# A decoder layer on one core: batch 0's shared expert in seven block products, and two sets of sums given out elsewhere

## The chip, the cores and the metric

The kernel runs on one core of a Trainium2 chip. The core has TensorE (PE, matrix products), VectorE (DVE), ScalarE (ACT) and GpSimd (POOL) for elementwise work, and queues of transfers that SyncE (SP), ScalarE and GpSimd issue. The metric is the device time of one execution in microseconds, as a median over several runs. The profile is of one more execution.

## The reference

A decoder layer on x of 4 batches x 512 tokens x 512 features, float32. Three blocks follow one another, each on the layer norm of x and added back to x:

```python
x = x + attention(_layernorm(x), wq, wk, wv, wo)       # 32 heads of 64, 8 key/value heads, causal
x = x + quantized_product(_layernorm(x), ctx_2048)     # both sides rounded to fp8 by blocks of 128
x = x + moe(_layernorm(x), Wg, W1, W3, W2, sw1, sw3, sw2)

def moe(xt, ...):                                      # xt: 2048 x 512
    probs = softmax(xt @ Wg)                           # 8 experts, the best one is taken
    # each expert takes its first 256 tokens, the rest are dropped
    h  = silu(xd @ W1[e]) * (xd @ W3[e])               # 512 -> 704, per expert
    oe = h @ W2[e]                                     # 704 -> 512
    shared = silu(xt @ sw1) * (xt @ sw3) @ sw2         # the same shape, for every token
    return gate * oe[slot] + shared
```

The change is in the last block only: the shared expert's upper part (silu(xt @ sw1) * (xt @ sw3)) and the sums around it.

## The kernel before

**Stages.** Attention of all four batches comes first (to about 1073 us). The quantized product and the routing of each batch are jobs that run beside it. Then comes the shared expert, batch by batch (to about 1300 us), with the last batch's quantized product and routing still beside it; then the eight experts (to 1532 us); then the last three pairs of shared lower products, beside which the experts' results are gathered and added.

**The shared expert.** Its upper part for batch b has six parts: chunks 0 to 4 of 128 hidden columns each (`HF` is 5), and a last one of 64 columns, here called (b,HF). `up` computes a chunk plainly: four products over k for sw1 into one PSUM bank and four for sw3 into another, each 128x128 by 128x512; then a silu on ScalarE and a product on VectorE. `up7` computes the same chunk in seven block products instead of eight, in the manner of Strassen and Winograd: the 2x2 blocks are (sw1, sw3) by halves of the 512 input features on the weights' side, and halves of the features by halves of the tokens on the other. A product has two matmuls 256 tokens wide. In order they are product 0 (a11 with b11), 1 (s2 with t2), 2 (s3 with t3), 3 (s1 with t1), 4 (a12 with b21), 5 (s4 with b22) and 6 (a22 with t4). VectorE joins them by seven additions, ScalarE copies one and takes two silus, and GpSimd multiplies the two results, called the gate product here.

The sums s1 to s4 of the weights come from `weight_sums` (four GpSimd instructions per chunk: s3, s1, s2, s4; s1 overwrites a21, the others go to `wS`, which is used again from expert to expert). The sums t1 to t4 of the tokens come from `token_sums` (GpSimd; for the last batch, t1, t2 and t4 on VectorE and t3 on GpSimd). In batch 0 every chunk is computed by `up`; after each, its weights' sums are formed for the batches behind it, and after chunk 2 the token sums of batch 1. `shared_down` computes 256 tokens of the lower part.

**Order of the work.** The schedule is manual: each engine executes what the program issues to it in that order. `units` lists the shared expert's units. Within a unit, `up`, `up7` and `down` call a function between their products (L1356, `between`), here called a stop: it advances the planner's clock `work.at` (1720 ns as a rule; 2500, 1700 and 1700 in `up7`) and then gives out steps of the jobs that are due. A job step that costs VectorE much names its price, and a stop has room for so much: 2.8 at the stops of `up` and `down`, and 1.3, 2.8 and 1.0 at the three of `up7`. Waits between steps are in units of `HALF`, 7250 ns of the planner's clock. A step marked "quiet" also waits until the planner reckons GpSimd done.

The jobs still open when the shared expert begins are, by the names of the code: r, m, n, o of the last heads (r broadcasts reciprocal row sums into `rrb` by a transfer, m and n multiply the heads' outputs aT by it on GpSimd in four instructions, and o is their output product, 16 matmuls, L408); c (rounding of the last batch's context, the transposes ptr_c); s and t (norm and quantized product of the last batch: a row h, a rounding, a transpose ptr_h, and four results y that GpSimd adds to acc); and w (the third norm, transposes ptr_h, router logits plg, the router, and four scatters of rows to `xd` by GpSimd). Expert e reads its 256 rows back from `xd` (`load_rows`, tile xe), transposes them (`turn_rows`, ptr_e) and forms their token sums (`expert_sums`).

**Experts.** For each of five chunks: `up7`, then `weight_sums` of the same chunk for the next expert; after chunk 1 the next expert's rows are turned, after chunk 2 its token sums are formed. Then `expert_rest` of the next expert (its 64-column part) and `down` of this one (products epy, chunk after chunk).

Of the kernel before, what the change touches and what calls it, by code (L numbers as in the profile page):

```python
# [11 lines left out]
ALU = mybir.AluOpType  # L12
# [11 lines left out]
def decoder_layer(  # L24
# [19 lines left out]
    B, T, D = x.shape  # L44
    HD = 64
    NQ = wq.shape[1] // HD
    E, _, H = W1.shape
# [7 lines left out]
    NHC = len(HCH)  # L55
# [39 lines left out]
    def bank(tag, name, dt=F32):  # L95
        bufs = {"sp": 4, "av": 1, "mm": 3}[tag]
        return psum.tile([P, 512], dt, tag=tag, bufs=bufs, name=name)
# [67 lines left out]
    def spin(n, name):  # L165
# [10 lines left out]
        out=mask[:, T - P : T],  # L176
# [19 lines left out]
        out=tri,  # L196
# [75 lines left out]
    def gpsimd(us, *args):  # L272
        nc.gpsimd.tensor_tensor(*args)  # L273
        work.gpsimd = max(work.gpsimd, work.at) + 1000 * us
# [474 lines left out]
    for b in range(B):  # L749
        z = b * SPB  # L750
# [329 lines left out]
    HF = H // P  # L1080
# [28 lines left out]
    se, h3x = {"next": 0}, {}  # L1109

    def load_h3(b):
        if b < B and b not in h3x and ("h3d", b) in over:
            h3x[b] = se[b % 2].tile([P, KC, T], F32, tag="h3x", name=f"h3x_{b}")
            bulk(out=h3x[b], in_=h3d[b])
# [17 lines left out]
    for d in range(len(todo)):  # L1132
# [12 lines left out]
        mid = work.spent  # L1145
# [12 lines left out]
    slots, evw = [], {}  # L1158
# [11 lines left out]
    gTs, xts = {}, {}  # L1170
# [6 lines left out]
    def up(w13, xT, gT, c, cols, name, mid=None):  # L1177


        at = (c * P, H + HT + c * P) if c < HF else (HF * P,)  # L1180
        ps = [bank("sp", f"p{m}_{name}") for m in range(len(at))]
        for pp, o in zip(ps, at):
            for k in range(KC):
                nc.tensor.matmul(  # L1184
                    pp[:, 0:cols],
                    w13[:, k, o : o + P],
                    xT[:, k, 0:cols],
                    start=(k == 0),
                    stop=(k == KC - 1),
                )  # L1190
                if mid and k % 2:
                    mid()
        g = gT[:, c, :]
        if c < HF:
            nc.scalar.activation(g, ps[0][:, 0:cols], AF.Silu)
            nc.vector.tensor_tensor(g, ps[1][:, 0:cols], g, ALU.mult)
            return

        nc.scalar.activation(g[HT:P, :], ps[0][0:HT, 0:cols], AF.Silu)
        gv = g.rearrange("p (a two t) -> p two a t", two=2, t=P)  # L1200
        pv = ps[0][:, 0:cols].rearrange("p (a two t) -> p two a t", two=2, t=P)
        nc.vector.tensor_tensor(gv[0:HT, 0], pv[HT:P, 0], gv[HT:P, 0], ALU.mult)
        nc.vector.tensor_tensor(gv[HT:P, 1], pv[HT:P, 1], gv[HT:P, 1], ALU.mult)
# [33 lines left out]
    xS = {}  # L1237

    def blocks(w, c):

        cols = slice(c * P, (c + 1) * P)
        low = slice(H + HT + c * P, H + HT + (c + 1) * P)
        return (
            w[:, 0:2, cols], w[:, 2:4, cols], w[:, 0:2, low], w[:, 2:4, low],
            *(wS[:, i, :, cols] for i in range(3)),
        )

    def weight_sums(w, c):

        a11, a12, a21, a22, s2, s3, s4 = blocks(w, c)  # L1250
        gpsimd(0.66, s3, a11, a21, ALU.subtract)
        gpsimd(0.66, a21, a21, a22, ALU.add)
        gpsimd(0.66, s2, a21, a11, ALU.subtract)
        gpsimd(0.66, s4, a12, s2, ALU.subtract)

    def token_sums(x, ts, cols, vector=False):

        half = cols // 2
        b11, b12, b21, b22 = (x[:, k : k + 2, t : t + half] for k in (0, 2) for t in (0, half))
        t1, t2, t3, t4 = ts  # L1260
        us = 1.27 * cols / T
        gpsimd(us, t3, b22, b12, ALU.subtract)
        for out, y, z in (t1, b12, b11), (t2, b22, t1), (t4, b21, t2):
            if vector:
                nc.vector.tensor_tensor(out, y, z, ALU.subtract)
            else:
                gpsimd(us, out, y, z, ALU.subtract)
        return t1, t2, t3, t4, b11, b21, b22

    def shared_sums(b):  # L1270
        xS[b] = token_sums(h3x[b], [xSs[:, i] for i in range(4)], T, b == B - 1)

    def up7(w, sums, g, c, cols, name, mid=None):
        a11, a12, s1, a22, s2, s3, s4 = blocks(w, c)
        t1, t2, t3, t4, b11, b21, b22 = sums
        half = cols // 2

        def product(i, w, x):
            ps = bank("av" if i == 3 else "sp", f"p7_{name}_{i}")[:, 0:half]
            for k in range(2):  # L1280
                nc.tensor.matmul(ps, w[:, k, :], x[:, k, :], start=k == 0, stop=k == 1)  # L1281
            return ps

        def part(tag, n=T // 2):
            return gp.tile([P, n], F32, tag=tag, bufs=2, name=f"{tag}_{name}")

        p1, u2, u3, c2 = part("p1"), part("u2"), part("u3"), part("c2", T)
        nc.scalar.copy(p1[:, 0:half], product(0, a11, b11))
        p1, u2, u3 = p1[:, 0:half], u2[:, 0:half], u3[:, 0:half]
        nc.vector.tensor_tensor(u2, product(1, s2, t2), p1, ALU.add)  # L1290
        nc.vector.tensor_tensor(u3, product(2, s3, t3), u2, ALU.add)
        if mid:
            mid(2500, 1.3)
        p5 = product(3, s1, t1)
        nc.vector.tensor_tensor(u2, p5, u2, ALU.add)
        nc.vector.tensor_tensor(c2[:, half:cols], p5, u3, ALU.add)
        nc.vector.tensor_tensor(g[:, 0:half], product(4, a12, b21), p1, ALU.add)
        if cols == T:
            nc.scalar.activation(g[:, 0:half], g[:, 0:half], AF.Silu)
        if mid:  # L1300
            mid(1700)
        nc.vector.tensor_tensor(g[:, half:cols], product(5, s4, b22), u2, ALU.add)
        lo = half if cols == T else 0
        nc.scalar.activation(g[:, lo:cols], g[:, lo:cols], AF.Silu)
        nc.vector.tensor_tensor(c2[:, 0:half], product(6, a22, t4), u3, ALU.add)
        gpsimd(1.27 * cols / T, g, g, c2[:, 0:cols], ALU.mult)
        if mid:
            mid(1700, 1.0)

    def shared_up(b, c, mid=None):  # L1310
        if b not in gTs:
            gTs[b] = gp.tile([P, NHC, T], F32, tag="gT", bufs=2, name=f"gT_{b}")
        if b and c < HF:
            up7(se["w"][0], xS[b], gTs[b][:, c, :], c, T, f"s{b}_{c}", mid)
        else:
            up(se["w"][0], h3x[b], gTs[b], c, T, f"s{b}_{c}", mid)
        if not b and c < HF:
            weight_sums(se["w"][0], c)
            if c == 2:
                shared_sums(1)  # L1320
        if c == (HF - 1 if b else HF):
            se["next"] = b + 2
            load_h3(b + 2)

# [22 lines left out]
    kept = set()  # L1347
    units = []
    for b in range(B):
        units += [(shared_up, b, c) for c in range(HF if b else NHC)]  # L1350
        units += [(shared_down, b, j) for j in range(0, TB, 2)]
        if b < B - 1:
            units.insert(-1, (shared_up, b + 1, HF))


    def between(ns=1720, room=2.8):  # L1356
        work.at += ns
        work.upto(n, 1e18, room)

    between()  # L1360
    while jobs or work.now:
        n += 1
# [20 lines left out]
    def load_w2(e):  # L1383
        if e < E:
            next(loads[e])
# [14 lines left out]
    def turn_rows(e):  # L1400
        if e < E:
            xTs[e] = h3x[B - 2][:, e % 2 * 2 : e % 2 * 2 + 2, :].rearrange(
                "p a (c t) -> p (a c) t", t=CAP
            )
            for t in range(CT):
                nc.scalar.copy(
                    xTs[e][:, :, t * P : (t + 1) * P],
                    transpose4(xes[e, t], f"ptr_e_{e}_{t}"),
                )
# [26 lines left out]
    units = [u for u in ups if u[2] == HF] + downs[:-3] + [u for u in ups if u[2] < HF]  # L1436
# [11 lines left out]
    units = downs[-3:]  # L1448
# [15 lines left out]
    for e in range(E):  # L1464
        for c in range(HF):
            up7(evw[e][0], exS[e], egTs[e][:, c, :], c, CAP, f"e{e}_{c}")
            if e < E - 1:
                weight_sums(evw[e + 1][0], c)
            if c == 1:
                turn_rows(e + 1)  # L1470
                load_rows(e + 2)
            if c == 2:
                expert_sums(e + 1)
        expert_rest(e + 1)
        load_e(e + 2)
        if e == E - 1:
            rows_back()
        for t, py in enumerate(down(egTs[e], evw[e][1], 0, f"epy_{e}", "mm")):
            yo = ep.tile([P, D], F32, tag="yo", bufs=2, name=f"yo_{e}_{t}")
            nc.vector.tensor_copy(yo, py)  # L1480
            r0 = e * CAP + t * P
            nc.sync.dma_start(out=oe[r0 : r0 + P, :], in_=yo)
        load_w2(e + 2)
# [96 lines left out]
```

## Time and profile before

| what | value |
|---|---|
| median of 3 runs | 1572.47 us (1570.51 to 1572.54) |
| profiled execution, its own time | 1569.79 us |
| span of that execution, first to last instruction | 1568.1 us |
| busy: TensorE, VectorE, ScalarE, GpSimd | 1530.8, 920.8, 535.1, 546.0 us |
| transferred | 194.42 MB, 124 GB/s on average |
| mean granted TensorE clock | 0.998 of full speed |

A row of a timeline is: start and length in us, engine, line (L273 is the helper through which all of GpSimd's elementwise instructions go), operation, output tile <- input tiles, shape, count; in brackets the idle time before it and what ended that. A 128x512 float32 product appears as two records. A stretch's row gives busy times of the five engines, the granted clock, the busy share of the transfer engines and GB/s.

### The profile page before, as it was taken

To read this page: it belongs to the slowest core of one execution; us is meant where nothing else is said; L and a number is where in the kernel's file an instruction comes from. 1 tells how busy PE (TensorE), PEld (TensorE's weight loads), DVE (VectorE), ACT (ScalarE), POOL (GpSimd) and SP (SyncE) were. 2 spreads that over 40 slices of the span, in tenths; PEclk is the share of its full clock that TensorE was granted. 3 is DMA by queue.
4 is the path that set the end of the run, shared out by engine and by line. 5 is a ranking of instruction groups with operands and counts; after the bars stand their busy time and mean duration, and the time that the engine had idled before them with its cause. 6 is when DMAs were issued, how large, how long until landed. Compare 5 with 4: busy or idle time off the path is not lost.

```text
span 1568.1 us, 22176 instructions
## 1 busy us (share of the span) xinstructions
PE 1530.8 (98%) x7324; PEld 890.5 (57%) x7324; DVE 920.8 (59%) x2732; ACT 535.1 (34%) x1611; POOL 546.0 (35%) x569
## 2 busy tenths in 40 slices
PE   9999999999999999999999999999999999999998
PEld 5455555455545545554555555555456867876873
DVE  4465843467776575887656495665665543443434
ACT  2354444334433434443444444452101221111110
POOL 2022301203334121334313133143445147776744
PEclk9999999999999999999999999999999999999999
DMA  4474430534234344423525342256051252655527
GB/s 142 129 222 148 101 101 21 158 105 102 79 84 142 88 123 140 102 88 75 146 84 133 118 114 61 61 159 191 19 210 54 81 193 76 208 178 184 191 90 260
DMA packets 118355, 194.42 MB, mean 124 GB/s; under 512 B 17120, under 2 KB 36576, under 8 KB 117728
## 3 DMA queue, kind: packets, MB, share of 16 engines
q10 hardware_dynamic: 65472, 100.94, 22.5%
q1 hardware_dynamic: 50208, 83.67, 17.6%
q0 software_dynamic: 2560, 8.39, 1.6%
q8 instruction: 58, 0.95, 0.3%
q14 instruction: 57, 0.47, 0.1%
HBM read 135.54 MB, written 28.05 MB: 104 GB/s over the span
## 4 chain that ended last, share of the span: by engine, by line
PE 69%; POOL 8%; DVE 2%; DMA 2%; issue 2%; ACT 1%; SPq 0%; ACTq 0%; POOLq 0%; DVEq 0%
PE py L408 12%; PE psq L308 10%; PE sc L939 7%; PE av L1020 7%; PE pt L989 6%; PE p_s L1281 5%; PE p_e L1281 5%; PE epy L1212 3%; PE p_s L1184 3%; PE psv L350 3%; POOL wS L273 3%; PE psk L308 3%; PE ys L1212 2%; POOL xS L273 1%; POOL slot_s L273 1%
## 5 line engine op out<-in xcount | busy, mean ns | idle before, releaser
L972 ACT ACTIVATE pm<-pm,mn 128x256 f32<-128x256 f32 (+3 forms) x512 | 281.0, 550 | 381.1 <-DVE mn L962 345.3
L962 DVE CUSTOM_DVE_ANT_0 pm<-sc,mask 128x256 f32<-128x256 f32 (+3 forms) x512 | 216.7, 485 | 91.4 <-PE sc L939 91.4
L408 PE MATMUL py<-wo,aT 128*128 128x512 f32 x512 | 239.2, 600 | 3.2 <-issue 2.0
L308 PE MATMUL psq<-hT,wq 128*128 128x512 f32 x512 | 236.5, 599 | 2.3 <-DVE y L604 2.3
L273 POOL TENSOR_TENSOR t1q<-t1q,tsq 128x512 f32<-128x512 f32 x64 | 83.9, 1312 | 391.1 <-DMA tsq<-t2q 154.1
L1006 DVE COPY pT<-pt 128x128 f32<-128x128 f32 (+3 forms) x256 | 114.2, 485 | 112.3 <-PE pt L989 104.0
L939 PE MATMUL sc<-kT,t1q 64*128 64x128 f32 (+3 forms) x1024 | 167.0, 451 | 6.8 <-ACT pT L1000 2.5
L989 PEld LDWEIGHTS pt<-ident,pm 128*128 128x128 f32 x1280 | 143.7, 141 | 36.2 <-issue 27.5
L989 PE MATMUL pt<-ident,pm 128*128 128x128 f32 x1280 | 154.4, 273 | 0.3 <-DVE mn L962 0.2
L1020 PE MATMUL av<-pT,v 128*64 128x512 f32 (+3 forms) x1024 | 152.3, 439 | 1.7 <-ACT pT L1000 1.7
L308 PEld LDWEIGHTS psq<-hT,wq 128*128 128x128 f32 x512 | 91.9, 190 | 102.1 <-issue 96.4
L1000 ACT COPY pT<-pt 128x128 f32<-128x128 f32 (+3 forms) x256 | 97.0, 430 | 147.6 <-PE pt L989 115.4
L408 PEld LDWEIGHTS py<-wo,aT 128*128 128x128 f32 x512 | 91.6, 190 | 97.8 <-issue 88.0
L939 PEld LDWEIGHTS sc<-kT,t1q 64*128 64x128 f32 x1024 | 86.4, 188 | 87.0 <-issue 58.3
L273 POOL TENSOR_TENSOR acc<-acc,y 128x512 f32<-128x512 f32 x64 | 81.0, 1270 | 153.3 <-DVE y L604 121.5
L1020 PEld LDWEIGHTS av<-pT,v 128*64 128x64 f32 x1024 | 68.3, 136 | 108.5 <-issue 96.4
L972 ACT ACTIVATION_READ_ACCUMULATOR pm<-pm,mn 128x1 f32 x512 | 95.7, 187 | 0.0
L273 POOL TENSOR_TENSOR aT<-aT,rrb 128x512 f32<-128x512 f32 x64 | 81.8, 1309 | 26.0 <-ACT pm L972 15.9
L1212 PE MATMUL epy<-slot_e,slot_s 128*128 128x512 f32 x160 | 71.8, 597 | 5.8 <-POOL slot_s L273 5.8
L1212 PE MATMUL ys<-slot_s,gT 128*128 128x512 f32 x160 | 71.7, 596 | 0.0
L416 DVE TENSOR_TENSOR acc<-py,acc 128x512 f32<-128x512 f32 x64 | 43.8, 686 | 46.3 <-PE py L408 45.6
L317 DVE TENSOR_TENSOR t2q<-psq,rt 128x512 f32<-128x512 f32 x64 | 44.0, 688 | 43.1 <-PE psq L308 40.2
(227 smaller groups left out, 2058.8 us busy)
## 6 DMA issues: line engine op xcount, KB each, us to landing
slot_e<-in_L_ffn_W_dram SPq DMA_DIRECT2D x14, 1280.0 KB
wq<-in_L_attn_wq_dram ACTq DMA_DIRECT2D x16, 1024.0 KB
tsq<-t2q SPq DMA_DIRECT2D x256, 64.0 KB
wo<-in_L_attn_wo_dram ACTq DMA_DIRECT2D x16, 1024.0 KB
rrb<-rrd ACTq DMA_DIRECT2D x32, 512.0 KB
slot_e<-in_L_ffn_W_dram SPq DMA_DIRECT2D x7, 1408.0 KB
kT<-t1k ACTq DMA_DIRECT2D x64, 128.0 KB
wv<-in_L_attn_wv_dram ACTq DMA_DIRECT2D x4, 1024.0 KB
```

Of the source, the lines that this page charges most:

```text
L273: nc.gpsimd.tensor_tensor(*args)
L308: nc.tensor.matmul(ps, w[:, k, c0 : c0 + P], hTs[b][:, k, :], start=(k == 0), stop=(k == KC - 1),)
L408: nc.tensor.matmul(py, aT[:, r, j * P : (j + 1) * P], wts["o", a][:, r, :], start=(r == 0), stop=(r == 3),)
L939: nc.tensor.matmul(scs[g][:, o : o + nk], qTs[b, p][g * HD : (g + 1) * HD, it * P : nk], kTs[b, p // 2][g * HD : (g + 1) * HD, 0:nk], star ...
L962: nc.vector.tensor_tensor_reduce(out=pm[:, o : o + nk], in0=scs[g][:, o : o + nk], in1=mask[:, T - nk : T], scale=-(HD**-0.5), scalar=3.0e ...
L972: nc.scalar.activation(pm[:, o : o + nk], pm[:, o : o + nk], AF.Exp, bias=mn, scale=-1.0, accum_out=rss[b, a][:, col : col + 1],)
L989: nc.tensor.transpose(pt[:, j * P : (j + 1) * P], pms[g][:, j * P : (j + 1) * P], ident)
L1000: nc.scalar.copy(pT[:, 0 : it + 1, it * P : nk], pt[:, o : o + nk].rearrange("p (j t) -> p j t", t=P),)
L1006: nc.vector.tensor_copy(pT[:, it + 1, 0:nk], pt[:, o : o + nk])
L1020: nc.tensor.matmul(av[g * HD : (g + 1) * HD, j * P : T], vs[b][:, j, v0 : v0 + HD], rhs, start=(j == 0), stop=(j == TB - 1),)
L1212: nc.tensor.matmul(py, gT[:, c, (t + i) * P : (t + i + 1) * P], w2[:, c, :], start=(c == 0), stop=False,)
L1281: nc.tensor.matmul(ps, w[:, k, :], x[:, k, :], start=k == 0, stop=k == 1)
```

## The change

Batch 0's chunks 1 to 4 are computed by `up7` too. For that its token sums are formed before the first unit (`shared_sums(0)`), and its units now run in the order chunk 0, (0,HF), 1, 2, 3, 4. Chunk 0 and (0,HF) stay plain. The weights' sums of chunks 1 and 2 are issued after (0,HF), those of chunk 3 after chunk 1, of chunk 4 after chunk 2, and of chunk 0 after chunk 3. The token sums of batch 1 move from behind chunk 2 to behind chunk 4. The load of batch 2's tokens follows chunk 4, again the last of the six. In the experts, the next expert's weights' sums of chunk c are issued after chunk c+1; those of chunks 3 and 4 both after chunk 4. In `token_sums`, t3 is formed third instead of first, and for the last batch on VectorE like the others.

```diff
@@ token_sums
         us = 1.27 * cols / T
-        gpsimd(us, t3, b22, b12, ALU.subtract)
-        for out, y, z in (t1, b12, b11), (t2, b22, t1), (t4, b21, t2):
+        for out, y, z in (t1, b12, b11), (t2, b22, t1), (t3, b22, b12), (t4, b21, t2):
             if vector:
                 nc.vector.tensor_tensor(out, y, z, ALU.subtract)
             else:
@@ shared_up
-        if b and c < HF:
-            up7(se["w"][0], xS[b], gTs[b][:, c, :], c, T, f"s{b}_{c}", mid)
+        w = se["w"][0]
+        if c == HF or (b, c) == (0, 0):
+            up(w, h3x[b], gTs[b], c, T, f"s{b}_{c}", mid)
         else:
-            up(se["w"][0], h3x[b], gTs[b], c, T, f"s{b}_{c}", mid)
-        if not b and c < HF:
-            weight_sums(se["w"][0], c)
-            if c == 2:
+            up7(w, xS[b], gTs[b][:, c, :], c, T, f"s{b}_{c}", mid)
+        if b == 0:
+
+            for k in {HF: (1, 2), 1: (3,), 2: (4,), 3: (0,)}.get(c, ()):
+                weight_sums(w, k)
+            if c == HF - 1:
                 shared_sums(1)
-        if c == (HF - 1 if b else HF):
+        if c == HF - 1:
             se["next"] = b + 2
             load_h3(b + 2)
@@ units
-        units += [(shared_up, b, c) for c in range(HF if b else NHC)]
+        units += [(shared_up, b, c) for c in (range(HF) if b else (0, HF, 1, 2, 3, 4))]
@@ before the first unit
+    shared_sums(0)
     between()
@@ experts
             up7(evw[e][0], exS[e], egTs[e][:, c, :], c, CAP, f"e{e}_{c}")
-            if e < E - 1:
-                weight_sums(evw[e + 1][0], c)
+
+            for k in (c - 1,) if c < HF - 1 else (HF - 2, HF - 1):
+                if e < E - 1 and k >= 0:
+                    weight_sums(evw[e + 1][0], k)
```

## The prediction

> **What bounds it.** Row 1 of the page: TensorE works 98% of the span. So the time is TensorE's work plus the few places where it waits, and those I looked for, in TensorE's timeline from 1060 us on and in the waits of the same stretch.
>
> ```profile
> PE 1530.8 (98%) x7324; PEld 890.5 (57%) x7324; DVE 920.8 (59%) x2732; ACT 535.1 (34%) x1611; POOL 546.0 (35%) x569
> ```
>
> Three kinds of wait can be touched. TensorE's timeline, start, length, instruction, idle before it:
>
> ```profile
> 1086.73 0.95 PE L655 MATMUL plg<-wg_sb,h3T 128*128 128x8 f32 x8
> 1087.54 0.64 PE L257 MATMUL ptr_h<-ident,h 128*128 128x128 f32 x4
> 1088.34 1.13 PE L408 MATMUL py<-wo,aT 128*128 128x512 f32 x2 [0.17 <-POOL aT L273]
> 1092.83 3.70 PE L408 MATMUL py<-wo,aT 128*128 128x512 f32 x8 [0.55 <-POOL aT L273]
> ...
> 1164.18 1.13 PE L1281 MATMUL p_s<-xS,wS 128*128 128x256 f32 x4 [2.58 <-DVE xt L1339]
> 1271.43 1.13 PE L1281 MATMUL p_s<-xS,wS 128*128 128x256 f32 x4 [1.36 <-POOL xS L273]
> 1350.03 3.60 PE L1212 MATMUL epy<-slot_e,slot_s 128*128 128x512 f32 x8
> 1354.44 5.42 PE L1212 MATMUL epy<-slot_e,slot_s 128*128 128x512 f32 x12 [0.82 <-POOL slot_s L273]
> ```
>
> A 128x512 product is two records. Back to back their starts are 0.4325 us apart (20 from 1208.34 to 1217.02); records of 128x256 are 0.216 apart (4 in 0.865). I measure waits by these pitches, since modelled ends overlap.
>
> GpSimd's timeline where batch 0's shared part begins, and in an expert:
>
> ```profile
> 1087.02 5.76 POOL L273 TENSOR_TENSOR aT<-aT,rrb 128x512 f32<-128x512 f32 x4 [10.05 <-DMA rrb<-rrd]
> 1092.74 1.16 POOL L273 TENSOR_TENSOR wS<-slot_s 128x256 f32<-128x256 f32 x1
> 1093.98 0.72 POOL L273 TENSOR_TENSOR slot_s<-slot_s 128x256 f32<-128x256 f32 x1
> 1094.79 0.72 POOL L273 TENSOR_TENSOR wS<-slot_s 128x256 f32<-128x256 f32 x1
> ...
> 1335.56 0.73 POOL L273 TENSOR_TENSOR slot_s<-slot_s,c_e 128x256 f32<-128x256 f32 x1 [7.24 <-ACT slot_s L1304]
> 1339.35 0.73 POOL L273 TENSOR_TENSOR slot_s<-slot_s,c_e 128x256 f32<-128x256 f32 x1
> 1353.67 0.72 POOL L273 TENSOR_TENSOR slot_s<-slot_s,c_e 128x256 f32<-128x256 f32 x1
> ```
>
> Its queue is strictly in order: chunk 0's weight sums, whose data were free since TensorE left chunk 0 at 1081.6, stand behind four aT products that wait for the rrb transfer until 1087.02.
>
> **1. Four chunks as block products.** Plain: 16 records x 0.4325 = 6.92 us. Seven products: 28 x 0.216 = 6.05. Saved 0.87 x 4 = **-3.5**. On VectorE each chunk goes from one 0.69 instruction to seven of 0.42; GpSimd gets a 1.27 product per chunk and token sums of 4 x 1.27 at the start. Those 5.1 us fit between the last av at 1073.5 and 1087.02, where GpSimd idles 10 us: nothing (without that cover, product 1 of chunk 1 would wait one for one). The VectorE work is priced in part 4.
>
> **2. A new wait.** Product 1 of chunk 1 needs s2 of chunk 1. Its sums are issued after (0,HF), and so behind the aT products: the planner gives those out at the fourth stop inside (0,0), before the change's first sums. TensorE: (0,0) ends at 1081.6, (0,HF) 8 records later at 1085.05, product 0 at 1085.9. GpSimd: rrb at 1087.02, four aT at 1.24 apart (the same four from 1032.67 took 4.97) to 1092.0, then s3, s1, s2, 0.80 + 0.80 + 0.72, to 1094.3. Wait: **+8.4**. Nothing on TensorE can pass: the output product o of the last heads (32 records, L408) comes at the planner's next stop, after product 2, since it is due 0.6 x 7250 ns after aT on the planner's clock and (0,HF) advances that by only 3440.
>
> [...] Before, a rounding on VectorE (L454, 1.64 instead of 0.69) ran beside aT, and aT took 5.76. [...] I take 8.4.
>
> In return o no longer waits for aT. From 1086.73 to 1106.27 TensorE did 0.80 + 0.51 + 13.84 + 0.22 + 1.3 + 0.8 = 17.4 us of work in 19.5: **-2.1**.
>
> **3. The clock.** A pause this long may lower TensorE's clock. The windows around the one dip of this trace (busy times of PE, PEld, DVE, ACT, POOL, then the granted clock):
>
> ```profile
> 350.00:355.00 5.00, 3.54 (x26) 2.40 (x24) 4.86 (x18) 4.90 (x17) 1.93 (x3) 0.96 0.24 56
> 355.00:360.00 5.00, 5.00 (x25) 3.21 (x26) 4.48 (x20) 3.28 (x14) 0.80 (x1) 0.70 0.02 5
> ```
>
> 0.04 x 5 + 0.30 x 5 = 1.7 us lost, after 1.5 us of idleness. [...] I take **+1.7**, a measured one.
>
> **4. The last batch's chain moves.** Block-product units have three stops with room 1.3, 2.8, 1.0 where plain ones have four of 2.8. Stepping the planner through both (its steps for before agree with where ptr_h, plg and py stand in the trace): t of the first token pair starts inside down(0,0) rather than in (0,4), its y in down(0,2)'s end and (1,0), and w(3) a whole unit later, its last step in (3,HF) rather than in down(2,0). The reasons: a rounding of c needs 2.4, and now finds only each unit's middle stop, so c ends at (0,4)'s first stop instead of (0,3)'s; t waits 7250 ns for c, and its own roundings, 2.7 each, then meet the units of batch 1 at one a unit. So the crowd on VectorE at 1146 to 1164 (eight y waiting for GpSimd's adds, then an h of 3.31 us) breaks up, and (1,0) no longer waits for a bank behind xt: **-2.6** (between -2.6 and 0). But the root, the router's first group, and three y at one stop now fall into units of seven VectorE instructions; such a root cost 0.33 at 1226.4. I take **+0.9** for all of them, from 0 to 2.6 at each place.
>
> Moved with the order: xS(1) goes after chunk 4, past the sums of chunks 3 and 4; it ends by about 1145 and is read at 1160. h3x(2)'s load still follows the last unit of batch 0. Chunk 3's s2 is ready about 3.7 us ahead of its product, chunk 4's 2.8.
>
> **5. t3 on VectorE.** At (3,0) product 2 could start at 1269.9 and started at 1271.43, since t3 stood on GpSimd behind four scatters. On VectorE it is 0.69 and done by 1268.8: -1.5. The router's last group now stands before (3,HF)'s gate product on VectorE, which frees a bank: 0.3. Net **-1.2**. The scatters start some 11 us later, at 1270 to 1271; expert 0's rows then land at 1286 to 1287, about when TensorE turns them (1286.6): nothing, and one for one if later.
>
> **6. Experts.** Before down's chunk 4, TensorE waits: eight records from 1350.03 end at 1353.49, the next starts at 1354.44: 0.95, seven times. After the change one chunk's sums (3.1 us) leave GpSimd's queue ahead of that last product, but not all is gained: between the first and second gate products GpSimd now idles, and chunk 2's inputs come at 1342.05 + 0.64 = 1342.7 (the lag of chunk 1: 1338.05 to 1338.69). From there 0.68 + 3.11 + 2.98 + 0.69 + 3.10 = 1353.25 against 1353.67: 0.42 x 7 = **-2.9**. The two sums given out behind chunk 4 have down and the 7.24 us of idleness as cover.
>
> **Sum:** -3.5 + 8.4 - 2.1 + 1.7 - 2.6 + 0.9 - 1.2 - 2.9 = **-1.3**. Against the profiled execution, 1569.79 (span 1568.1), 1568.5; that execution stands 2.68 below the median of 1572.47, so on the median's footing **1571.2**. 0.2%, 3.1 us, is what a measurement here tells from no change.
>
> **Rivals.** *Slower, 1577 (0.30):* VectorE is late in the block-product units of batches 0 and 1, and each time the third product waits for its bank 2.6 us as at 1161.6. For it: seven instructions against one, with the chain beside them; against it: (1,1) to (1,4) ran with the chain and no wait. The old wait kept and two such new ones: -1.3 - 0.9 + 3 x 2.6 = +5.6, less if they are partial; from 4.4 us of them on it decides. *Faster, 1562.6 (0.12):* the sums of chunk 1 are not behind aT, or rrb lands by 1079: -8.4 - 1.7 + 2.1 more, -9.3 in all, roughly 1563. Against it: the order of GpSimd's queue. *Faster, 1567.4 (0.08):* the experts' wait goes whole, 6.7 for 2.9. *The products save nothing, 1574.7 (0.04):* PSUM or weight loads eat the saving; (1,1), from 1168.60 to 1174.65 without a wait, speaks against it.
>
> **Numbers.** My case has 0.46, its own range 1568.5 to 1574.5, 0.04 of it faster. Faster 0.04 + 0.12 + 0.08 = 0.24; same 0.42 + 0.04 = 0.46; slower 0.30. The range 1566 to 1578 leaves about one in ten on each side.
>
> **What would show it.** A wait of TensorE for POOL wS of about 8 us near 1086 and a clock under 1 after it; o without waits for aT; no wait at (1,0); t3 among VectorE's token sums and the wait at (3,0) gone; epy's waits near 0.4 instead of 0.8. No wait near 1086, or several for DVE between 1120 and 1200, would make me wrong.

## The result, and the profile after

| | before | after |
|---|---|---|
| median of 14 runs each | 1571.88 us (1569.66 to 1574.49) | 1570.39 us (1568.38 to 1575.5) |
| profiled execution | 1569.79 us, span 1568.1 | 1570.42 us, span 1568.7 |
| TensorE's mean granted clock | 0.998 | 0.994 |

After to before: 0.9993, with a 95% interval of 0.9985 to 1.0002. No difference can be told. But much has moved inside, and nearly cancelled.

The first row of the page, kernel after; busy us, share of the span and number of instructions of each engine:

```profile
PE 1529.6 (98%) x7372; PEld 901.4 (57%) x7372; DVE 924.2 (59%) x2757; ACT 537.3 (34%) x1619; POOL 554.7 (35%) x576
```

TensorE's share is 98% as before, so this row shows nothing of what happened. TensorE's timeline does. Kernel after; columns as before (start, length, instruction, and in brackets the idle time and what ended it):

```profile
1085.94 1.03 PE L1280 MATMUL p_s<-h3x,slot_s 128*128 128x256 f32 x4
1094.72 3.78 PE L1280 MATMUL p_s<-xS,wS 128*128 128x256 f32 x8 [7.75 <-POOL wS L273]
1098.29 1.71 PE L655 MATMUL plg<-wg_sb,h3T 128*128 128x8 f32 x8
1099.86 1.09 PE L257 MATMUL ptr_h<-ident,h 128*128 128x128 f32 x4
1100.74 7.63 PE L408 MATMUL py<-wo,aT 128*128 128x512 f32 x14
...
1142.02 3.60 PE L1212 MATMUL ys<-slot_s,gT 128*128 128x512 f32 x8
1146.62 5.42 PE L1212 MATMUL ys<-slot_s,gT 128*128 128x512 f32 x12 [1.00 <-POOL gT L273]
...
1167.28 1.13 PE L1280 MATMUL p_s<-h3x,slot_s 128*128 128x256 f32 x4
1168.25 1.89 PE L1280 MATMUL p_s<-xS,wS 128*128 128x256 f32 x8
1275.25 1.03 PE L1280 MATMUL p_s<-h3x,slot_s 128*128 128x256 f32 x4
1276.11 1.89 PE L1280 MATMUL p_s<-xS,wS 128*128 128x256 f32 x8
1326.30 3.60 PE L1212 MATMUL epy<-slot_e,slot_s 128*128 128x512 f32 x8
1330.17 5.42 PE L1212 MATMUL epy<-slot_e,slot_s 128*128 128x512 f32 x12 [0.27 <-POOL slot_s L273]
```

Read it from the top. Product 0 of chunk 1 runs, then TensorE waits for GpSimd's weight sums: the new wait. The next eight records take 3.78 us where eight such take 1.89 elsewhere: half speed. The output product o (py) has lost its waits for aT. down(0,0) has a new wait of 1.0. At (1,0), from 1167.28, and at (3,0), from 1275.25, the products follow one another without the waits for xt and xS. The expert's wait is less than half of what it was: the eight records from 1326.30 end at 1326.30 + 8 x 0.4325 = 1329.76, so the wait is 0.41 instead of 0.95.

GpSimd's timeline of the kernel after says why TensorE waits:

```profile
1087.45 4.92 POOL L273 TENSOR_TENSOR aT<-aT,rrb 128x512 f32<-128x512 f32 x4 [5.79 <-DMA rrb<-rrd]
1092.34 0.72 POOL L273 TENSOR_TENSOR wS<-slot_s 128x256 f32<-128x256 f32 x1
1093.14 0.72 POOL L273 TENSOR_TENSOR slot_s<-slot_s 128x256 f32<-128x256 f32 x1
1093.94 0.72 POOL L273 TENSOR_TENSOR wS<-slot_s 128x256 f32<-128x256 f32 x1
```

The three sums that product 1 depends on (s2 is the third, and is formed from the second) stand behind the aT products, for which GpSimd idled 5.79 us until a transfer landed. s2 ends at 1094.66, and product 1 starts at 1094.72. The windows around it, kernel after (busy time of PE, PEld, DVE, ACT, POOL, granted clock, transfer share, GB/s):

```profile
1085.00:1090.00 5.00, 1.97 (x7) 0.95 (x5) 1.51 (x3) 0.96 (x2) 2.54 (x3) 1.00 0.56 153
1090.00:1095.00 5.00, 0.28 (x1) 0.28 (x2) 0.00 (x0) 0.00 (x0) 4.76 (x6) 0.50 0.00 0
1095.00:1100.00 5.00, 5.00 (x17) 4.28 (x17) 0.85 (x2) 0.00 (x0) 4.32 (x6) 0.50 0.00 2
1100.00:1105.00 5.00, 5.00 (x12) 2.66 (x12) 0.17 (x1) 0.59 (x1) 0.00 (x0) 0.63 0.18 52
```

The clock falls to a half while TensorE waits and stays there after it works again. Finer windows put the half rate from 1090.02 to 1103.67. The last 9.0 us of that are work, which at half rate costs an estimated 4.5 us.

Where the time went, from the starts of the same instructions in both traces. The "later" column is the shift of the kernel after against the kernel before, both counted from the start of (0,0):

| start of | before | after | later | forecast up to here |
|---|---|---|---|---|
| (0,0) | 1073.45 | 1074.43 | 0 | 0 |
| down(0,0) | +60.47 | +67.59 | +7.1 | +4.5 |
| (1,0) | +86.16 | +92.85 | +6.7 | |
| (3,HF) | +191.19 | +197.28 | +6.1 | |
| the first expert's 64-column part | +227.45 | +231.91 | +4.5 | +1.6 |
| the last expert's down | +448.95 | +449.56 | +0.6 | -1.3 |

The start of (0,0) is itself 1.0 us later in this execution, and the part after the last row is 1.0 shorter.

### The profile page after: what moved, and what is told of

Read it like the earlier page. It is cut to its first block, busy times and chain, and to the rows that moved or that the text cites. A ratio compares the mean times of both kernels' runs of the same rounds, so it can differ in the third digit from the quotient of the medians.

```text
span 1568.7 us, 22346 instructions
## 1 busy us (share of the span) xinstructions
PE 1529.6 (98%) x7372; PEld 901.4 (57%) x7372; DVE 924.2 (59%) x2757; ACT 537.3 (34%) x1619; POOL 554.7 (35%) x576
## 4 chain that ended last, share of the span: by engine, by line
PE 77%; POOL 7%; DVE 5%; DMA 5%; issue 3%; ACT 2%; SPq 1%; ACTq 0%; POOLq 0%; DVEq 0%
PE py L408 14%; PE psq L308 12%; PE sc L939 8%; PE av L1020 8%; PE pt L989 7%; PE p_s L1280 6%; PE p_e L1280 5%; PE psv L350 4%; PE psk L308 3%; PE ys L1212 3%; PE epy L1212 2%; POOL wS L273 2%; DMA tsq<-t2q 2%; ACT pm L972 1%; PE ptr_h L257 1%
## 5 line engine op out<-in xcount | busy, mean ns | idle before, releaser
L939 PE MATMUL sc<-kT,t1q 64*128 64x384 f32 (+3 forms) x1024 | 165.8, 448 | 7.5 <-ACT pT L1000 3.0
```

The costliest lines, as they stand in the source:

```text
L939: nc.tensor.matmul(scs[g][:, o : o + nk], qTs[b, p][g * HD : (g + 1) * HD, it * P : nk], kTs[b, p // 2][g * HD : (g + 1) * HD, 0:nk], star ...
```

## The experiments

The theory, A in the expectations: the change holds two gains (the two sets of sums given out elsewhere, in the experts and for the last tokens) and one loss (the wait at chunk 1 of batch 0 with the half clock behind it), and they cancel. If so, each half alone must move the time, in opposite directions, and the loss must go away when its cause does. The rivals, by their letters in the expectations: that the sums only move a wait elsewhere, or that the block products alone make nothing slower (B), that VectorE's backlog holds the time (C), that TensorE's idleness brings no further loss than the wait itself (D), and, on the clock, two different reasons for how long it stays low (E and F). All ratios are to the kernel before, with 95% intervals.

**The two sets of sums, without batch 0's block products.** The kernel before, with the experts' order and the token sums of after:

```diff
 token_sums
-        gpsimd(us, t3, b22, b12, ALU.subtract)
-        for out, y, z in (t1, b12, b11), (t2, b22, t1), (t4, b21, t2):
+        for out, y, z in (t1, b12, b11), (t2, b22, t1), (t3, b22, b12), (t4, b21, t2):
 experts
-            if e < E - 1:
-                weight_sums(evw[e + 1][0], c)
+            for k in (c - 1,) if c < HF - 1 else (HF - 2, HF - 1):
+                if e < E - 1 and k >= 0:
+                    weight_sums(evw[e + 1][0], k)
```

> The kernel before with the experts' weight sums a part later and t3 of the last tokens on VectorE; batch 0 stays plain. Theory A (the change is two gains and one loss that cancel; the loss sits at the start of chunk 1 of batch 0): 3.9 us from the experts (seven waits of 0.95 become 0.41, by the pitch of the records) and 1.5 from t3, so 5.4 us under before, ratio 0.9966. Rival B (GpSimd's later sums only move the wait elsewhere in the experts): under 2 us.

Measured: 1564.58 us, 0.9960 (0.9947 to 0.9973). These two parts gain 6.3 us, interval 4.2 to 8.3. Rival B, under 2 us, is out. The forecast had 4.1 for them.

**Batch 0's block products alone.** The kernel after, with the same two places put back (the diff above, reversed).

> The changed kernel with the experts' order and t3 as they were before: only batch 0's four chunks in block products, with their sums. Theory A: the wait of TensorE for GpSimd's sums (7.9 us), and 4.5 us lost to the half clock behind it, less 3.5 saved by the products, less 2.1 of waits for aT, less about 1 where the last batch's work no longer crowds VectorE: 4 to 6 us over before, ratio about 1.003. Rival B: no slower than before, since then what the change gains would be here and not in the sums.

Measured: 1574.49 us, 1.0018 (1.0011 to 1.0026): 2.8 us lost, interval 1.7 to 4.1. Rival B, no slower than before, is out here too. But it is below the 4 to 6 us expected, whose lower end the interval only just reaches. The forecast's parts 1 to 4 add up to -3.5 + 8.4 - 2.1 + 1.7 - 2.6 + 0.9 = +2.8. The wait in this kernel's TensorE timeline, and its windows:

```profile
1095.97 3.78 PE L1281 MATMUL p_s<-xS,wS 128*128 128x256 f32 x8 [7.97 <-POOL wS L273]
1099.54 1.38 PE L655 MATMUL plg<-wg_sb,h3T 128*128 128x8 f32 x8
```

```profile
1095.00:1100.00 5.00, 4.03 (x11) 3.32 (x12) 0.64 (x2) 0.00 (x0) 4.61 (x8) 0.50 0.01 2
1100.00:1105.00 5.00, 5.00 (x19) 2.97 (x20) 0.48 (x3) 0.59 (x1) 0.81 (x1) 0.96 0.20 52
```

The wait is nearly the same (8.1 us by the pitch of the records, against 7.9), but the clock is back at 1100.43: 4.5 us of work at half rate instead of 9.0 (the expectation further down has it as 4.4). The expectation here had been made from the 9.0. Added up, the two halves give -6.3 + 2.8 = -3.5 where the whole gave -1.1 by its ratio (-2.4 to +0.3). The gap of 2.4 lies just inside what the three intervals allow together.

**The cause of the wait taken away.** Kernel after, with the weight sums of chunk 1 issued before the first unit, and so ahead of the aT products that wait for the transfer:

```diff
     shared_sums(0)
+    busy_until = work.gpsimd
+    weight_sums(se["w"][0], 1)
+    work.gpsimd = busy_until
     between()
 shared_up
-            for k in {HF: (1, 2), 1: (3,), 2: (4,), 3: (0,)}.get(c, ()):
+            for k in {HF: (2,), 1: (3,), 2: (4,), 3: (0,)}.get(c, ()):
```

(The planner's figure for GpSimd is put back, so that the order of the other jobs stays the same.)

> The changed kernel with the weights' sums of chunk 1 issued before the first unit, ahead of the aT products in GpSimd's queue; the planner's clock for GpSimd is left as it was, so that everything else keeps its place. Theory A: no wait at product 1 and no dip of the clock: 7.9 + 4.5 less 1 to 2 us of waits for aT that return in o: 10 to 11 us under the changed kernel, 11 to 12 under before, ratio about 0.993. Rival C (VectorE's backlog in batches 0 and 1 holds the time): under 4 us gained, since the wait would come back behind the units that follow.

Measured: 1559.58 us, 0.9923 (0.9910 to 0.9935). That is 10.8 below the kernel after and 11.9 (10.2 to 14.1 by the interval) below before. GpSimd's timeline of this kernel:

```profile
1081.76 0.73 POOL L273 TENSOR_TENSOR wS<-slot_s 128x256 f32<-128x256 f32 x1
1082.56 0.73 POOL L273 TENSOR_TENSOR slot_s<-slot_s 128x256 f32<-128x256 f32 x1
1083.37 0.72 POOL L273 TENSOR_TENSOR wS<-slot_s 128x256 f32<-128x256 f32 x1
...
1088.59 4.95 POOL L273 TENSOR_TENSOR aT<-aT,rrb 128x512 f32<-128x512 f32 x4 [2.69 <-DMA rrb<-rrd]
```

And TensorE's:

```profile
1087.07 1.03 PE L1280 MATMUL p_s<-h3x,slot_s 128*128 128x256 f32 x4
1087.94 1.89 PE L1280 MATMUL p_s<-xS,wS 128*128 128x256 f32 x8
...
1090.94 6.34 PE L408 MATMUL py<-wo,aT 128*128 128x512 f32 x14
```

The sums now fill idle time ahead of the transfer, aT starts when rrb lands as before, the eight records take 1.89, and o still has no wait. The clock is 1.00 in all windows from 1085 to 1105. So the position in GpSimd's queue was the whole cause of the wait and of the half clock, and rival C, under 4 us, is out. In this kernel (0,0) to down(0,0) takes 55.36 us, 5.1 less than in the kernel before: the -3.5 and -2.1 of the forecast, nearly. It is 12.2 less than in the profiled execution of the kernel after, more than the 10.8 between the medians; that execution had the longest half rate of those profiled. The expectation reached its 10 to 11 another way: it took off 1 to 2 us for waits in o, which did not come back.

**The wait kept, TensorE kept busy through it.** Kernel after, with nine more products behind product 0 of chunk 1, into a bank that nobody reads:

```diff
+        if name == "s0_1":
+            idle = bank("mm", "idle")
+            for _ in range(9):
+                nc.tensor.matmul(idle, a11[:, 0, :], h3x[0][:, 0, :], start=True, stop=True)
```

> The changed kernel with nine extra products (128x512, their result is not read) behind product 0 of chunk 1, so that TensorE works through the wait for GpSimd's sums; the wait itself stays. It tells the wait from the clock. Theory A: the granted clock stays at 1 and 4 to 4.5 us come back, ratio to before 0.9965 to 0.997. Rival D (the recorded dip costs nothing real, or the wait alone is the loss): the time of the changed kernel, within 1 us.

Measured: 1565.41 us, 0.9960 (0.9948 to 0.9972), 5.0 below after. TensorE's timeline of this kernel, and a window in it:

```profile
1087.50 7.89 PE L1291 MATMUL idle<-h3x,slot_s 128*128 128x512 f32 x18
1095.64 1.99 PE L1280 MATMUL p_s<-xS,wS 128*128 128x256 f32 x8 [0.25 <-POOL wS L273]
```

```profile
1090.00:1095.00 5.00, 5.00 (x13) 2.09 (x11) 0.00 (x0) 0.00 (x0) 4.84 (x6) 1.00 0.00 0
```

From the end of product 0 to product 1 it is 8.1 us, about as long as in the kernel after (7.9). But the clock stays at 1.00, and rival D is out. The idleness of the kernel after costs twice: 7.9 us as the wait, and behind it the half rate, an estimated 4.5 us by the trace and 5.0 by the medians.

**How long the clock stays low.** The kernel after showed 9.0 us of work at half rate, the kernel with the block products alone 4.5. One idea, E in the expectation, was that what runs first after the wait decides: narrow matmuls (plg and ptr_h, which stood right behind it) would hold the clock down. So the first stop of chunk 1 was moved behind two more products:

```diff
 up7
-        if mid:
+        if mid and name != "s0_1":
             mid(2500, 1.3)
...
+        if name == "s0_1":
+            mid(2500, 1.3)
```

> The changed kernel with the first stop of chunk 1 moved behind products 3 and 4, so that after the wait TensorE has four wide block products (5.2 us at half rate) ahead of the router's narrow products (8 columns) and transposes. Theory E (narrow products do not count as work for the clock: the half rate lasted 9.0 us after the wait in the changed kernel, where 1.6 us of them fell into the second stretch of 3.4 us, and 4.4 us in blocks_only, where they came later): half rate ends within 3.4 to 6.8 us after the wait, about 2 us under the changed kernel. Rival F (only the position of a free-running window decides): a duration as in the changed kernel is as likely as a shorter one, and no difference in the time over many runs.

Measured: 1570.49 us, 0.9990 (0.9983 to 0.9996), against 0.9993 for the kernel after: the 2 us that E expected are not seen. In its profile 5.2 us of work, from 1094.37 to 1099.52, ran at half rate:

```profile
1094.37 3.78 PE L1280 MATMUL p_s<-xS,wS 128*128 128x256 f32 x8 [8.09 <-POOL wS L273]
```

```profile
1095.00:1100.00 5.00, 5.00 (x14) 4.04 (x13) 1.06 (x3) 0.00 (x0) 3.97 (x6) 0.55 0.00 2
```

The other idea, F, a guess that no trace had shown, was that nothing of the kernel decides, only where the wait happens to fall in time. For that the kernel after was profiled once more, unchanged:

> The changed kernel once more, for the duration of the half clock after the wait: Theory E expects 3 or 4 stretches of 3.4 us again, by where the wait falls; under rival F it may be two as well.

Measured: 1567.88 us in this one execution. TensorE's timeline and windows in it:

```profile
1094.23 3.78 PE L1280 MATMUL p_s<-xS,wS 128*128 128x256 f32 x8 [8.07 <-POOL wS L273]
1097.81 1.21 PE L655 MATMUL plg<-wg_sb,h3T 128*128 128x8 f32 x8
```

```profile
1090.00:1095.00 5.00, 0.77 (x2) 0.68 (x3) 0.00 (x0) 0.00 (x0) 4.76 (x7) 0.65 0.00 0
1095.00:1100.00 5.00, 5.00 (x22) 4.10 (x21) 1.01 (x3) 0.46 (x1) 3.83 (x5) 0.67 0.00 2
1100.00:1105.00 5.00, 5.00 (x13) 2.17 (x12) 0.69 (x1) 0.12 (x1) 0.00 (x0) 1.00 0.20 52
```

The same kernel, 4.1 us at half rate instead of 9.0. This execution is not a typical one: it was faster than all 14 of the kernel after, and its clock, as a mean over the whole execution, is 0.997, above all of theirs (0.991 to 0.995). All these traces have the same TensorE work between product 1 of chunk 1 and down(0,0), so that stretch prices the clock:

| kernel | product 1 of chunk 1 to down(0,0) | more than with TensorE kept busy | half rate after the wait |
|---|---|---|---|
| kept busy | 42.91 us | 0 | none |
| after, again | 44.91 | 2.0 | 4.1 us |
| block products alone | 45.09 | 2.2 | 4.5 |
| first stop later | 45.69 | 2.8 | 5.2 |
| after | 47.30 | 4.4 | 9.0 |

The loss is half the time at half rate, to within 0.2 us in every row. The same program gave both ends of the table, 4.1 and 9.0 us at half rate, so something besides the program decides, which fits F without showing what it is. E's forecast for this execution, 3 or 4 stretches of 3.4 us, failed: it has two.

But the 9.0 stands apart in one more way. The dips last 13.65, 6.83, 10.24 and 10.24 us (after, again, block products alone, first stop later): 4, 2, 3 and 3 steps of 3.41. Count the steps from the start of each dip. In three of the traces the clock came back at the end of the first whole step after the restart. In the kernel after that step is 1096.85 to 1100.26, TensorE worked all through it, and the clock stayed at a half for one step more. It is also the step with the most narrow work, 1.97 us of plg and ptr_h; the same step of the others has 0.50 (again, 1094.90 to 1098.31), 0.89 (block products alone, 1097.02 to 1100.43) and none (first stop later, 1096.11 to 1099.52). E and F together fit all four traces. But that was read off afterwards, from a single long dip, and no run tests it.

**The experts' order alone**, and **the token sums alone**, on the kernel before:

> The kernel before with only the experts' weight sums a part later. Theory A: 0.54 us less at each of seven waits ahead of down's chunk 4 (0.95 to 0.41), 3.8 us, ratio 0.9976; with t3_only it adds up to what both gave together. The forecast's own figure was 2.9 us, from 0.42 a wait.

> The kernel before with only t3 of the last tokens on VectorE (and third in order). Theory A: the 1.5 us of waiting at product 2 of (3,0) go, ratio 0.999, at the edge of what five rounds tell; in the trace product 2 follows product 1 at once. Rival: the wait turns up at the next bank, nothing in time.

Measured: 1567.15 us, 0.9968 (0.9957 to 0.9979), or -5.0, for the experts' order; 1570.01 us, 0.9985 (0.9977 to 0.9992), or -2.4 (-3.6 to -1.3), for the token sums, by the ratios. Both lie above what was expected (3.8 and 1.5), which their intervals still hold. They make -7.4 together, where both in one kernel gave -6.3 (-8.3 to -4.2). TensorE's timeline of the kernel with the experts' order alone:

```profile
1325.76 3.60 PE L1212 MATMUL epy<-slot_e,slot_s 128*128 128x512 f32 x8
1329.74 5.42 PE L1212 MATMUL epy<-slot_e,slot_s 128*128 128x512 f32 x12 [0.38 <-POOL slot_s L273]
```

The eight records end at 1325.76 + 3.46 = 1329.22; the wait is 0.52 and was 0.95. That is 0.43 saved, against the forecast's 0.42, and 3.0 over seven waits. So the expectation's 0.54 was wrong for this edit alone, and of the 5.0 measured (3.3 to 6.8) the trace accounts for about 3; the rest is not explained. In the kernel after it is 0.41, 0.11 less, because the token sums in their new order take 2.87 us from first to last instead of 2.98. In the kernel with the token sums alone the wait at (3,0) is gone:

```profile
1269.20 1.03 PE L1280 MATMUL p_s<-h3x,slot_s 128*128 128x256 f32 x4
1270.07 1.89 PE L1280 MATMUL p_s<-xS,wS 128*128 128x256 f32 x8
```

**Further along the same line.** On the version with early sums, the experts' sums of chunks 0 and 1 stay one part late, and those of chunk 2 wait for chunk 4 too:

```diff
-            for k in (c - 1,) if c < HF - 1 else (HF - 2, HF - 1):
+            for k in {1: (0,), 2: (1,), 4: (2, 3, 4)}.get(c, ()):
```

> early_sums with the experts' weight sums of chunk 2 behind chunk 4 as well, so that three chunks' sums (9.3 us) stand behind the last gate product. If GpSimd's queue is all that holds down's chunk 4, the remaining seven waits of 0.41 go, 2.9 us under early_sums, 1556.7, ratio to before about 0.9905. Rival: 9.3 us of sums run into the next expert's first gate product and token sums, and the wait comes back there or at the last gate product of the next expert: the time of early_sums.

Measured: 1556.95 us, 0.9906 (0.9892 to 0.9920). No expert waits in its down any more (two records of chunk 4 follow on chunk 3's):

```profile
1314.12 8.75 PE L1212 MATMUL epy<-slot_e,slot_s 128*128 128x512 f32 x20
```

What was left, besides, was the 1.0 in down(0,0). There the root of the last batch's norm stands on VectorE before the two additions of (0,4) that the gate product needs. On top of the version just shown, the stop that gives it out was moved behind those two:

```diff
 up7
-        if mid:
+        if mid and name != "s0_4":
             mid(1700)
...
+        if name == "s0_4":
+            mid(1700)
```

> sums_two_later with the middle stop of (0,4) moved behind the two additions on VectorE that end that chunk, ahead of its gate product, so that the norm's root (13 small instructions) no longer stands between product 5 and the gate product. Theory (the new wait of 1.0 us in down(0,0) is VectorE's: root, then the addition, then ScalarE's silu, then GpSimd's gate product): the wait goes, 1 us under sums_two_later, seen in the trace more than in the time. Rival (GpSimd's own queue holds the gate product): the wait stays.

Measured: 1554.78 us, 0.9888 (0.9873 to 0.9904). TensorE's timeline of this kernel:

```profile
1131.46 8.83 PE L1212 MATMUL ys<-slot_s,gT 128*128 128x512 f32 x20
...
1149.36 0.40 PE L257 MATMUL ptr_h<-ident_b,qq_x 128*128 128x128 bf16 x4 [0.95 <-DVE qq_x L456]
...
1152.70 0.40 PE L257 MATMUL ptr_h<-ident_b,qq_x 128*128 128x128 bf16 x4 [0.31 <-DVE qq_x L456]
```

The wait in down(0,0) is gone, and 0.95 + 0.31 us have come up at the next reader of the delayed chain, with 0.25 more inside (0,4). From the start of (0,0) to the last expert's down this trace is 0.4 us longer than that of the version before it (434.08 against 433.65), so its trace shows no gain. The medians say 2.2 less, but the intervals overlap, and what this last edit is worth is not settled. By its median this is the fastest version, 17 us or 1.1% below the kernel before.

## Why the prediction was right, point by point

The time forecast was 1571.2 us, no measurable change. It came out so with most of the mechanism as described. But the terms for the clock (+1.7, measured 2.0 to 4.4) and for the experts (-2.9, measured -3.9) were too small, in opposite directions, and others were off by 0.4 to 0.7. That the sum came within 1 us of the measured time is luck in part.

**Part 1, block products, -3.5: right in mechanism.** With the wait out of the way, the stretch from (0,0) to down(0,0) lost 5.1 us against parts 1 and 2's -3.5 - 2.1 = -5.6. The pitch of the products after is the 0.216 that the working used.

**Part 2, the wait, +8.4: right in place, cause and size.** Product 0 ended at 1086.80 by its pitch, product 1 started at 1094.72: 7.9. The choice of 8.4 was right as well. In the kernel after, VectorE ran nothing from 1087.63 to 1096.90, so no rounding stood beside the four aT products, and they took 4.92 us (1.23 each), as in the row from 1032.67 (4.97), where VectorE ran other instructions. They took 5.76 in the kernel before, where the last batch's rounding (L449 to L456, 1087.81 to 1093.32, L454 with 1.64 instead of 0.69) ran beside them. No run here changes that alone, so why they took longer is not shown. Taking the sums off their place behind aT removed the wait whole. The -2.1 for o came as forecast: no wait for aT is left.

**Part 3, the clock, +1.7: the mis-sized term.** It measured 4.4 us in the execution profiled first, and 2.0, 2.2 and 2.8 in three others. By the medians it is 10.8 - 7.9 = 2.9 from the version with early sums, or 5.0 from the one kept busy, each uncertain by some 2 us. The working took over the price of another dip, one after 1.5 us of idleness: 3.4 us at half rate, all of it behind the pause, where TensorE works. At chunk 1 the clock was at a half (0.50) when TensorE resumed, in all four traces with that wait (7.9 to 8.3 us), and what lay behind the wait was not 3.4 us but 4.1, 4.5, 5.2 and 9.0. So all four losses are above 1.7. In the kernel after, the clock stayed at a half through the whole step from 1096.85 to 1100.26, in which TensorE worked throughout, and for one step more; the row of the other dip, with its single step, could not show that.

**Part 4, the chain, -2.6 + 0.9: right in mechanism, -1.0 instead of -1.7.** The chain's order is as forecast (w(3) a unit later, its last step in (3,HF)), and the wait at (1,0) is gone whole. The backlog on VectorE cost more than 0.9: by the pitch of the records, 1.1 in down(0,0) and 1.0 ahead of 1183.46 (1.0 and 0.8 in the brackets), less 0.4 of an old wait for y, at 1153.10, that went. With the 2.7 that went at (1,0) this makes the -1.0. VectorE and GpSimd in the kernel after show the first:

```profile
1144.16 0.16 DVE L247 SCALAR_TENSOR_TENSOR rsb<-r0b,rsb 128x4 f32<-128x4 f32 x1
1144.24 0.42 DVE L1301 TENSOR_TENSOR gT<-p_s,u_s 128x256 f32<-128x256 f32 x1
```

```profile
1145.18 1.38 POOL L273 TENSOR_TENSOR gT<-gT,c_s 128x512 f32<-128x512 f32 x1 [2.73 <-ACT gT L1303]
```

The root's last instruction is at 1144.16, then the addition at 1144.24, a silu, and the gate product at 1145.18, which down waits for. The forecast named the root in a block-product unit, and priced it by a place where the reader was a free bank (0.33) and not the next stage.

**Part 5, t3, -1.2: -1.6.** The wait went whole and the scatters started at 1277.27 instead of 1259.54, 17.7 later, of which some 7 are the shift of everything. The forecast had 11 later. They delayed nobody.

**Part 6, the experts, -2.9: -3.9 in the trace.** The 0.42 per expert is right for the order alone (0.43). The other 0.11 x 7 = 0.8 is the term that was overlooked: the change also reorders the token sums, which every expert forms, and only part 5 was credited with that edit. In the trace of the token sums alone it is less: six of the seven waits are 0.87 and one is 1.16, 0.3 saved in all, which with the 1.6 at (3,0) makes about 2 of the 2.4 measured.

**The rivals.** The slower one (VectorE late in the block units, 1577) did not come: such waits were 1.0 and 0.8, not twice or three times 2.6. The one with sums not behind aT, 1562.6, is just what the version with early sums made, and that gave 1559.6. The difference is mainly the larger gain of the sums. The other two did not come either: the experts' wait did not go whole (0.41 is left), and the products did save their 3.5. Put together by the trace of the kernel after: 7.9 - 3.5 - 2.1 + 4.5 = +6.8 (+7.1 seen), -1.0, -1.6, -3.9, in all +0.6 or so, and +0.6 is the difference of the two profiled executions, in which the 1.0 at the start and the 1.0 at the end cancel.

**Still open:** why the half rate lasted 9.0 us behind the wait in one execution, when a wait at nearly the same place and of nearly the same length left 4.1, 4.5 and 5.2 in three others. Narrow work in the step at whose end the clock came back in those three is the best candidate, untested.

## What to carry to other kernels

GpSimd executed its instructions in the order of issue here: chunk 1's sums started at 1092.34 where they were issued behind the aT products that waited for a transfer, and at 1081.76 where they were issued ahead of them. So work that is ready is to be issued ahead of an instruction that waits. Here four small sums behind such an instruction, rather than ahead of it, decided between no gain and 11 us. The waits of 7.9 to 8.3 us cost TensorE their length plus half of the low-clock time behind them (2.0 to 4.4 us for 4.1 to 9.0), and work that filled the wait, though nobody read it, kept the clock at 1.00 and took the second part away. An edit to a shared helper is to be priced at every caller, and a stall that is cleared is to be looked for at the next reader of what was delayed.

## What was not expected of the hardware

The time at half rate was not proportional to the wait. The dips looked at here lasted 3.4, 6.8, 10.2 or 13.65 us, steps of 3.41: 6.8 to 13.65 for TensorE's waits at chunk 1, which are 7.9 to 8.3 us by the pitch of the records, and 3.4 for a pause of 1.46 us early in the kernel before (to 354.33), with a clock of 0.70 from 355 to 360. A shorter wait did not always bring one: the same pause in the kernel after (to 356.71) brought none, with 1.00 from 350 to 365. Nor did the wait of 2.6 us at (1,0) in the kernel before, where the clock is 1.00 from 1160 to 1170. The same wait, 2.6 to 2.7 us, brought one with the two sets of sums and with the experts' order alone: the first four records behind it took 1.84 and 1.75 us there, where their pitch makes it 0.865.

On GpSimd, a token sum that uses the result just before it started 0.80 to 0.81 us behind it, and one that does not 0.69. The token sums t1 to t4 of an expert and the gate product behind them, kernel after:

```profile
1322.74 0.73 POOL L273 TENSOR_TENSOR xS<-h3x 128x256 f32<-128x256 f32 x1
1323.55 0.73 POOL L273 TENSOR_TENSOR xS<-h3x,xS 128x256 f32<-128x256 f32 x1
1324.24 0.73 POOL L273 TENSOR_TENSOR xS<-h3x 128x256 f32<-128x256 f32 x1
1324.93 0.72 POOL L273 TENSOR_TENSOR xS<-h3x,xS 128x256 f32<-128x256 f32 x1
1325.61 0.72 POOL L273 TENSOR_TENSOR slot_s<-slot_s,c_e 128x256 f32<-128x256 f32 x1
```

Here t2 is formed from t1 and starts 0.81 us behind it. t3, t4 and the gate product do not use the result just before them, and start 0.68 to 0.69 behind. In the old order, t3, t1, t2, t4, both t2 and t4 follow the sum that they are formed from, and both start 0.80 behind it (kernel before). So the new order takes 0.11 us less with the same four instructions.
